# Self-attention over four images on one core: exponentials without a shift, taken straight from PSUM, and the next image's projection woven between the pairs

## The chip, the cores and the metric

The kernel runs on one core of one Trainium2 chip. The metric is the device time of one execution in microseconds (us). The engines are named as the profile names them: PE is TensorE's matmul side and PEld its weight loads, DVE is VectorE, ACT is ScalarE, POOL is GpSimd, SP is SyncE, which here only issues DMAs.

## What is computed

For each of B = 4 images of 64 x 64 pixels with 256 channels, in float32:

```python
q = einsum('bwhc,cd->bwhd', x, Wq) + bq      # d = 128
k = einsum('bwhc,cd->bwhd', x, Wk) + bk      # d = 128
v = einsum('bwhc,cd->bwhd', x, Wv) + bv      # d = 256
pq, pk, pv = (t.reshape(B, -1, N) for t in (q, k, v))   # N = 4096
energy = einsum('bcn,bcm->bnm', pq, pk)      # 4096 x 4096 per image
attention = softmax(energy, axis=-1)
out = einsum('bcm,bnm->bcn', pv, attention).reshape(x.shape)
return gamma * out + x
```

The reshapes do not transpose: an image's flat memory is cut into 128 rows (256 for v) of 4096 columns.

## The kernel before

An image's 4096 query columns n are cut into 8 groups of 512, and the 4096 key columns m into 32 blocks of 128. Two neighbouring blocks are a pair, so that there are 16 pairs in a group and 128 in an image (`STEPS`), 512 in all. The kernel's functions, with their lines:

- `project` (L107) makes pq, pk and pvT of one image in 16 steps. A step turns four 128 x 128 pieces of x (`transposed`, L119), copies them to SBUF on ACT (xts, L123), multiplies them by Wq and Wk (qk, L134), adds the biases on DVE (L142), multiplies by Wv in two halves (v, L152), and after each half lets ACT add the bias while it copies (pvT, L159). All four images do this ahead of their pairs; pq, pk and pvT have one buffer each.
- `energy` (L184) computes one pair's energies, transposed, 128 m by 512 n in each of two banks (s, L188), and ACT copies them to SBUF (p, L196).
- `running_max` (L206) and `column_max` (L210) find the largest energy of each n: a running maximum over the 16 pairs on DVE, then four transposes (mt, L216), a reduction (L218), a diagonal (L220), and a matmul with ones that spreads the result over all partitions (sb, L228), which ACT copies (shift, L232).
- `exponent` (L234) subtracts the shift on DVE in place (L237) and takes the exponential on ACT in place (L240).
- `running_sum` (L242) adds up the exponentials on DVE (ssum, L250), `attend` (L252) multiplies them by pvT into two accumulators (o, L263).
- `finish` (L273) copies the accumulators (L277, L278), adds the two halves of ssum (z, L280), spreads the sum with a matmul of ones (zb, L283), takes reciprocals (L287), scales (L290), and lets POOL add x (L293); SP loads that x (xr) and stores the result (L294).

The order of the work is written out by hand (L296 to L318), and every engine works through its own list in order. Since a group's maximum needs all its energies, energies run `LEAD` = 18 pairs ahead of attention: an image begins with 18 pairs of energies alone, then each step issues energies 18 pairs ahead, the exponential two pairs ahead, the sum, the maximum, and attention. `column_max` and `finish` are generators; `proceed` pushes each of them on by one piece twice in a step. A float32 matmul stands in the trace as two MATMUL instructions.

Of the kernel before, what the change touches and what calls it, by code (L numbers as in the profile page):

```python
# [8 lines left out]
F32 = mybir.dt.float32  # L9
AF = mybir.ActivationFunctionType  # L10
# [6 lines left out]
def kernel(  # L17
# [25 lines left out]

    nc = tc.nc
    B, W, H, C = x.shape
    P = 128
# [7 lines left out]
    KC = C // P  # L54
    STEPS = NG * NP
    LOOK = 2
    LEAD = NP + LOOK
# [11 lines left out]
    xpool = ctx.enter_context(tc.tile_pool(name="xpool", bufs=2))  # L69
    rpool = ctx.enter_context(tc.tile_pool(name="rpool", bufs=2))  # L70
    qkv = ctx.enter_context(tc.tile_pool(name="qkv", bufs=1))
    ppool = ctx.enter_context(tc.tile_pool(name="ppool", bufs=LEAD + 2))
    xtpool = ctx.enter_context(tc.tile_pool(name="xtpool", bufs=2))
    work = ctx.enter_context(tc.tile_pool(name="work", bufs=1))
    stat = ctx.enter_context(tc.tile_pool(name="stat", bufs=2))
    ps_s = ctx.enter_context(tc.tile_pool(name="ps_s", bufs=2, space=PSUM))
    ps_t = ctx.enter_context(tc.tile_pool(name="ps_t", bufs=2, space=PSUM))
    ps_o = ctx.enter_context(tc.tile_pool(name="ps_o", bufs=1, space=PSUM))

    ctx.enter_context(tc.manual_schedule())  # L80

    def load_x(b, g):
        t = xpool.tile([P, 2, NB], F32, tag="x", name=f"x_{b}_{g}")
        nc.sync.dma_start(t, xv[b, g])
        return t

    first = [load_x(0, 0)]
# [19 lines left out]
    def project(b, xs):  # L107
        pq = qkv.tile([P, NM, P], F32, tag="pq", name=f"pq_{b}")
        pk = qkv.tile([P, NM, P], F32, tag="pk", name=f"pk_{b}")
        pvT = qkv.tile([P, NM, C], F32, tag="pvT", name=f"pvT_{b}")  # L110
        def transposed(i):

            g, o = i // 2, (i % 2) * C
            if i % 2 == 0 and len(xs) == g + 1 < NG:
                xs.append(load_x(b, g + 1))
            tp = ps_t.tile([P, KC, 2, P], F32, tag="t", name=f"xt_{b}_{i}")
            for k in range(KC):
                for s in range(2):
                    nc.tensor.transpose(  # L119
                        tp[:, k, s, :], xs[g][:, s, o + k * P : o + (k + 1) * P], ident  # L120
                    )
            xt = xtpool.tile([P, KC, 2, P], F32, tag="xt", name=f"xts_{b}_{i}")
            nc.scalar.copy(xt, tp)  # L123
            return xt

        following = transposed(0)
        for i in range(NM // 2):
            xt = following
            if i + 1 < NM // 2:
                following = transposed(i + 1)  # L130
            qk = ps_s.tile([P, 2, 2 * C2], F32, tag="s", name=f"qk_{b}_{i}")
            for s in range(2):
                for k in range(KC):
                    nc.tensor.matmul(  # L134
                        qk[:, s, :],
                        xt[:, k, s, :],
                        wqk_sb[:, k, :],
                        start=(k == 0),
                        stop=(k == KC - 1),
                    )  # L140
            for dst, o in ((pq, 0), (pk, C2)):
# [7 lines left out]
            vp = ps_o.tile([P, KC, C], F32, tag=f"o{i % 2}", name=f"v_{b}_{i}")  # L149
            for eh in range(KC):  # L150
                for k in range(KC):
# [3 lines left out]
                        xt[:, k].rearrange("p s a -> p (s a)"),  # L155
                        start=(k == 0),
                        stop=(k == KC - 1),
                    )
                nc.scalar.activation(  # L159
                    pvT[:, 2 * i + eh, :],  # L160
# [4 lines left out]
        return pq, pk, pvT  # L165

    for b in range(B):
        pq, pk, pvT = project(b, first)
        pqf = pq.rearrange("p j d -> p (j d)")
        pairs = {}  # L170
        shift = {}
        ssum = {}
# [10 lines left out]

        def energy(step):  # L184
            g, t = divmod(step, NP)
            sp = ps_s.tile([P, 2, NB], F32, tag="s", name=f"s_{b}_{step}")
            for h in range(2):
                nc.tensor.matmul(  # L188
                    sp[:, h, :],
                    pk[:, 2 * t + h, :],  # L190
                    pqf[:, g * NB : (g + 1) * NB],
                    start=True,
                    stop=True,
                )
            p = ppool.tile([P, 2, NB], F32, tag="p", name=f"p_{b}_{step}")
            nc.scalar.copy(p, sp)  # L196
            pairs[step] = p

        def running_max(step):
            g, t = divmod(step, NP)  # L200
            p = pairs[step]
            if t == 0:
                running_max.mx = work.tile([P, 2, NB], F32, tag="mx", name=f"mx_{b}_{g}")
            else:
                q = pairs[step - 1] if t == 1 else running_max.mx
                nc.vector.tensor_tensor(running_max.mx, q, p, ALU.max)  # L206
            if t == NP - 1:
                start(column_max(g, running_max.mx))

        def column_max(g, mx):  # L210
            m1 = work.tile([P, NB], F32, tag="m1", name=f"m1_{b}_{g}")
            nc.vector.tensor_tensor(m1, mx[:, 0, :], mx[:, 1, :], ALU.max)
            yield
            tp = ps_t.tile([P, NJ, P], F32, tag="t", name=f"mt_{b}_{g}")
            for j in range(NJ):
                nc.tensor.transpose(tp[:, j, :], m1[:, j * P : (j + 1) * P], ident)  # L216
            cm = stat.tile([P, NJ], F32, tag="cm", name=f"cm_{b}_{g}")
            nc.vector.tensor_reduce(cm, tp, AX.X, ALU.max)  # L218
            diag = work.tile([P, NJ, P], F32, tag="m1", name=f"diag_{b}_{g}")
            nc.vector.tensor_tensor(  # L220
                diag,
                ident.unsqueeze(1).to_broadcast([P, NJ, P]),
                cm.unsqueeze(2).to_broadcast([P, NJ, P]),
                ALU.mult,
            )
            yield
            sb = ps_t.tile([P, NB], F32, tag="t", name=f"sb_{b}_{g}")
            nc.tensor.matmul(  # L228
                sb, ones, diag.rearrange("p j n -> p (j n)"), start=True, stop=True
            )  # L230
            shift[g] = stat.tile([P, NB], F32, tag="shift", name=f"shift_{b}_{g}")
            nc.scalar.copy(shift[g], sb)  # L232

        def exponent(step):  # L234
            g, t = divmod(step, NP)
            p = pairs[step]
            nc.vector.tensor_tensor(  # L237
                p, p, shift[g].unsqueeze(1).to_broadcast([P, 2, NB]), ALU.subtract
            )
            nc.scalar.activation(p, p, AF.Exp)  # L240

        def running_sum(step):  # L242
            g, t = divmod(step, NP)
            p = pairs[step]
            if t == 0:
                ssum[g] = work.tile([P, 2, NB], F32, tag="ssum", name=f"ssum_{b}_{g}")
            elif t == 1:
                nc.vector.tensor_tensor(ssum[g], pairs[step - 1], p, ALU.add)  # L248
            else:
                nc.vector.tensor_tensor(ssum[g], ssum[g], p, ALU.add)  # L250

        def attend(step):  # L252
            g, t = divmod(step, NP)
            if t == 0:
                attend.acc = [
# [3 lines left out]
            p = pairs[step]  # L259
            for h in range(2):  # L260
                m = 2 * t + h
                for s in range(2):
                    nc.tensor.matmul(  # L263
                        attend.acc[s],
                        pvT[:, m, s * P : (s + 1) * P],
                        p[:, h, :],
# [3 lines left out]
            if t == NP - 1:  # L270
                start(finish(g, attend.acc))

        def finish(g, acc):  # L273
# [6 lines left out]
            nc.vector.tensor_tensor(z, ssum[g][:, 0, :], ssum[g][:, 1, :], ALU.add)  # L280
            yield
            zb = ps_t.tile([P, NB], F32, tag="t", name=f"zb_{b}_{g}")
            nc.tensor.matmul(zb, ones, z, start=True, stop=True)  # L283
            r = work.tile([P, NB], F32, tag="r", name=f"r_{b}_{g}")
# [4 lines left out]
            for s in range(2):  # L289
                nc.vector.scalar_tensor_tensor(  # L290
                    o[:, s, :], o[:, s, :], gam, r, ALU.mult, ALU.mult
                )
            nc.gpsimd.tensor_tensor(xr, xr, o, ALU.add)  # L293
            nc.sync.dma_start(ov[b, g], xr)  # L294

        for step in range(LEAD):  # L296
            energy(step)
            running_max(step)
            proceed()
        while active:  # L300
            proceed()
        exponent(0)
        exponent(1)
        for step in range(STEPS):
            if step + LEAD < STEPS:
                energy(step + LEAD)
            proceed()
            if step + 2 < STEPS:
                exponent(step + 2)
            running_sum(step)  # L310
            if step + LEAD < STEPS:
                running_max(step + LEAD)
            attend(step)
            proceed()
            if step == STEPS - NP and b + 1 < B:
                first = [load_x(b + 1, 0)]
# [32 lines left out]
```

## Time and profile before

| | |
|---|---|
| median of 3 runs | 3162.92 us (3161.79 to 3163.8) |
| the profiled execution | 3163.9 us, span 3162.1 us |
| mean granted clock of TensorE | 0.990 |
| HBM traffic over the span | 34.21 MB read, 16.78 MB written, 16 GB/s |

The span runs from the first to the last instruction; the time lies 1.8 us above it. Granted clock is the share of full speed that TensorE was given. A row of the profile names the line, the engine, the operation, what it writes and reads, the shape, how often, and after a bar the busy time, the mean of one in ns and the idle time of that engine just before it. In a timeline a row is: start, length, engine, line, and in brackets the idle time before it and who ended it.

### The profile page before, as it was taken

Reading aid. Unit: us, or ns where it says so; the run is one execution under the profiler, and the core shown is the slowest. Engines: PE = TensorE matmul, PEld = TensorE weight load, DVE = VectorE, ACT = ScalarE, POOL = GpSimd, SP = SyncE. Lnnn points to the kernel's source line nnn. Section 1 sums busy time; section 2 is a strip of 40 time slices with the busy share of each in tenths; the row PEclk is TensorE's granted clock in tenths of the full one; section 3 lists DMA queues with packets and bytes.
Section 4 is the critical chain, followed back from the end, with each engine's and each line's share of the span. In section 5 each row is a group of like instructions: output and inputs, shape, how many; then the busy total and the mean of one; then the engine's idle time right before and its main releaser. Section 6 shows DMA issues by size and latency. Waiting matters only on the chain.

```text
span 3162.1 us, 20027 instructions
## 1 busy us (share of the span) xinstructions
PE 3006.7 (95%) x7680; PEld 1424.0 (45%) x7680; DVE 2070.7 (65%) x1889; ACT 1158.0 (37%) x1281; POOL 149.9 (5%) x38
## 2 busy tenths in 40 slices
PE   8999999999899999999989999999998999999998
PEld 6444444444644444444464444444446444444443
DVE  1577777776167777777715777777771677777776
ACT  3433333332243333333224333333322433333332
POOL 0000000000000000000000000000000000000000
PEclk9999999999999999999999999999999999999999
DMA  2000000000100000000010000000001000000000
GB/s 69 1 13 10 4 14 14 14 14 20 60 1 14 14 0 14 13 14 14 20 60 0 14 14 0 14 14 13 14 20 60 0 14 13 14 0 14 14 14 20
DMA packets 27743, 52.26 MB, mean 17 GB/s; under 512 B 2048, under 2 KB 3072, under 8 KB 27648
## 3 DMA queue, kind: packets, MB, share of 16 engines
q1 hardware_dynamic: 26112, 50.34, 5.0%
q8 instruction: 60, 0.98, 0.1%
q10 hardware_dynamic: 1536, 0.66, 0.1%
q14 instruction: 35, 0.29, 0.0%
HBM read 34.21 MB, written 16.78 MB: 16 GB/s over the span
## 4 chain that ended last, share of the span: by engine, by line
PE 94%; DVE 3%; ACT 1%; DMA 1%; issue 0%; POOL 0%; POOLq 0%; SPq 0%; DVEq 0%; ACTq 0%
PE o L263 56%; PE s L188 28%; PE v L152 4%; PE qk L134 4%; PE zb L283 1%; PE sb L228 1%; ACT pvT L159 1%; PE xt L119 1%; DVE osb L278 1%; DMA x<-in_x_dram 1%; DVE z L280 1%; PE mt L216 0%; DVE r L287 0%; DVE mx L206 0%; ACT p L196 0%
## 5 line engine op out<-in xcount | busy, mean ns | idle before, releaser
L263 PE MATMUL o<-p,pvT 128*128 128x512 f32 x4096 | 1837.5, 594 | 11.5 <-ACT p L240 11.5
L263 PEld LDWEIGHTS o<-p,pvT 128*128 128x128 f32 x4096 | 780.2, 191 | 996.0 <-issue 981.3
L196 ACT COPY p<-s 128x1024 f32<-128x1024 f32 x512 | 518.2, 1012 | 1430.7 <-PE s L188 1417.8
L188 PE MATMUL s<-pq,pk 128*128 128x512 f32 x2048 | 957.3, 595 | 0.0
L206 DVE TENSOR_TENSOR mx<-mx,p 128x1024 f32<-128x1024 f32 x448 | 565.2, 1262 | 526.4 <-ACT p L196 523.6
L237 DVE TENSOR_TENSOR p<-p,shift 128x1024 f32<-128x1024 f32 x512 | 621.8, 1216 | 52.7 <-ACT shift L232 52.7
L240 ACT ACTIVATE p<-p 128x1024 f32<-128x1024 f32 x512 | 542.5, 1060 | 204.2 <-DVE p L237 200.6
L188 PEld LDWEIGHTS s<-pq,pk 128*128 128x128 f32 x2048 | 388.7, 191 | 477.2 <-issue 460.5
L250 DVE TENSOR_TENSOR ssum<-ssum,p 128x1024 f32<-128x1024 f32 x448 | 546.0, 1219 | 0.8
L293 POOL TENSOR_TENSOR xr<-xr,osb 128x1024 f32<-128x1024 f32 x32 | 149.2, 4661 | 3007.7 <-DVE osb L290 3007.7
L142 DVE TENSOR_TENSOR pq<-qk,bqk_sb 128x256 f32<-128x256 f32 x64 | 27.2, 425 | 270.5 <-PE qk L134 270.5
L152 PE MATMUL v<-xts,wv_sb 128*128 128x256 f32 x512 | 139.0, 394 | 36.1 <-ACT pvT L159 36.1
L159 ACT ACTIVATE pvT<-v,bv_sb 128x256 f32<-128x256 f32 x128 | 60.8, 475 | 210.4 <-PE v L152 210.4
L287 DVE RECIPROCAL r<-zb 128x256 f32<-128x256 f32 x64 | 107.8, 1726 | 40.7 <-PE zb L283 40.7
L134 PE MATMUL qk<-wqk_sb,xts 128*128 128x256 f32 x512 | 126.5, 392 | 0.2 <-ACT xts L123 0.2
L152 PEld LDWEIGHTS v<-xts,wv_sb 128*128 128x128 f32 x512 | 93.0, 191 | 72.2 <-ACT pvT L159 61.8
L134 PEld LDWEIGHTS qk<-wqk_sb,xts 128*128 128x128 f32 x512 | 96.3, 198 | 12.0 <-ACT xts L123 0.6
L206 DVE TENSOR_TENSOR mx<-p,p 128x1024 f32<-128x1024 f32 x32 | 39.2, 1225 | 69.5 <-ACT p L196 69.5
L278 DVE COPY osb<-o 128x512 f32<-128x512 f32 x32 | 22.1, 692 | 94.2 <-PE o L263 94.2
L283 PE MATMUL zb<-z,ones 128*128 128x512 f32 x64 | 35.2, 631 | 48.9 <-DVE z L280 48.9
L248 DVE TENSOR_TENSOR ssum<-p,p 128x1024 f32<-128x1024 f32 x32 | 75.8, 2368 | 0.0
L119 PE MATMUL xt<-ident,x 128*128 128x128 f32 x256 | 40.8, 285 | 28.9 <-DMA x<-in_x_dram 26.9
(23 smaller groups left out, 360.9 us busy)
## 6 DMA issues: line engine op xcount, KB each, us to landing
x<-in_x_dram SPq DMA_DIRECT2D x32, 512.0 KB, 4.0
xr<-in_x_dram SPq DMA_DIRECT2D x32, 512.0 KB, 4.6
out_dram<-xr SPq DMA_DIRECT2D x32, 512.0 KB, 3.5
wv_sb<-in_L_conv_Wv_dram ACTq DMA_DIRECT2D x1, 256.0 KB, 6.9
wqk_sb<-in_L_conv_Wq_dram ACTq DMA_DIRECT2D x1, 128.0 KB, 2.2
wqk_sb<-in_L_conv_Wk_dram ACTq DMA_DIRECT2D x1, 128.0 KB, 5.0
bqk_sb<-in_L_conv_bq_dram ACTq DMA_DIRECT2D x1, 64.0 KB, 6.5
bqk_sb<-in_L_conv_bk_dram ACTq DMA_DIRECT2D x1, 64.0 KB, 6.1
```

The costliest lines, as they stand in the source:

```text
L134: nc.tensor.matmul(qk[:, s, :], xt[:, k, s, :], wqk_sb[:, k, :], start=(k == 0), stop=(k == KC - 1),)
L152: nc.tensor.matmul(vp[:, eh, :], wv_sb[:, k, eh * P : (eh + 1) * P], xt[:, k].rearrange("p s a -> p (s a)"), start=(k == 0), stop=(k == KC ...
L159: nc.scalar.activation(pvT[:, 2 * i + eh, :], vp[:, eh, :], AF.Identity, bias=bv_sb[:, eh : eh + 1],)
L188: nc.tensor.matmul(sp[:, h, :], pk[:, 2 * t + h, :], pqf[:, g * NB : (g + 1) * NB], start=True, stop=True,)
L196: nc.scalar.copy(p, sp)
L206: nc.vector.tensor_tensor(running_max.mx, q, p, ALU.max)
L237: nc.vector.tensor_tensor(p, p, shift[g].unsqueeze(1).to_broadcast([P, 2, NB]), ALU.subtract)
L240: nc.scalar.activation(p, p, AF.Exp)
L250: nc.vector.tensor_tensor(ssum[g], ssum[g], p, ALU.add)
L263: nc.tensor.matmul(attend.acc[s], pvT[:, m, s * P : (s + 1) * P], p[:, h, :], start=(m == 0), stop=(m == NM - 1),)
L287: nc.vector.reciprocal(r[:, sl], zb[:, sl])
L293: nc.gpsimd.tensor_tensor(xr, xr, o, ALU.add)
```

## The change

The new kernel makes four edits to the order and adds a second path.

1. `energy` takes the exponential of the unshifted energies on ACT, from PSUM into p. The copy, the maximum, the subtraction and `column_max` are gone; energies run `LOOK` = 2 pairs ahead; p has 5 buffers for 20.
2. Projection becomes a class. Image 0 is projected whole; images 1 to 3 in pieces (four transposes and the copy; qk and its adds; v and its activations), one after attention of each pair whose number in the image is 2, 4 or 6 modulo 7, so 48 pieces in 112 of 128 pairs. pq, pk and pvT have two buffers. All projection tiles use `ps_t` in PSUM (two slots), as zb does. Both halves of v come ahead of both activations. The pairs of all four images run through as one loop.
3. `finish` gives its matmul later by one piece, keeps the lowest and highest sum in zmin and zmax, scales in one instruction, and stores from POOL's queue.
4. After the pairs a flag is made: is a sum under 2^-60 or over 2^80? If so, a general path (with the maximum, as before, but unwoven) does everything again.

```diff
+    Z_LOW, Z_HIGH = 2.0**-60, 2.0**80
...
-            p = ppool.tile([P, 2, NB], F32, tag="p", name=f"p_{b}_{step}")
-            nc.scalar.copy(p, sp)
+            p = ppool.tile([P, 2, NB], F32, tag="p", name=f"p_{step}")
+            nc.scalar.activation(p, sp, AF.Exp)
...
         def v(self, i):
             pool, tag = self.psum
             vp = pool.tile([P, KC, C], F32, tag=tag, name=f"v_{self.b}_{i}")
             for eh in range(KC):
                 for k in range(KC):
                     nc.tensor.matmul(...)
+            for eh in range(KC):
                 nc.scalar.activation(
                     self.pvT[:, 2 * i + eh, :], vp[:, eh, :], AF.Identity, ...)
...
+        def whole(self):
+            self.transposed(0)
+            for i in range(NI):
+                if i + 1 < NI:
+                    self.transposed(i + 1)
+                self.qk(i)
+                self.v(i)
+
+        def pieces(self):
+            for i in range(NI):
+                self.transposed(i)
+                yield
+                self.qk(i)
+                yield
+                self.v(i)
+                yield
...
+        xpool, rpool, xtpool = pool("xpool", 2), pool("rpool", 2), pool("xtpool", 2)
+        qkv, ppool, work = pool("qkv", 2), pool("ppool", LOOK + 3), pool("work", 1)
+        ps_s = pool("ps_s", 2, space=PSUM)
+        ps_t = pool("ps_t", 2, space=PSUM)
+        ps_o = pool("ps_o", 1, space=PSUM)
...
             nc.vector.tensor_tensor(z, ssum[:, 0, :], ssum[:, 1, :], ALU.add)
             yield
+            yield
             zb = ps_t.tile([P, NB], F32, tag="t", name=f"zb_{b}_{g}")
             nc.tensor.matmul(zb, ones, z, start=True, stop=True)
+            yield
+            nc.vector.tensor_tensor(zmin, zmin, zb, ALU.min)
+            nc.vector.tensor_tensor(zmax, zmax, zb, ALU.max)
...
             nc.gpsimd.tensor_tensor(xr, xr, o, ALU.add)
-            nc.sync.dma_start(ov[b, g], xr)
+            nc.gpsimd.dma_start(ov[b, g], xr)
...
+        for step in range(LOOK):
+            energy(step)
+        for step in range(B * STEPS):
+            r = step % STEPS
+            if r == 0:
+                ahead = following(step // STEPS + 1)
+            if step + LOOK < B * STEPS:
+                energy(step + LOOK)
+            proceed()
+            running_sum(step)
+            attend(step)
+            proceed()
+
+            if r % 7 in (2, 4, 6):
+                next(ahead, None)
+        while active:
+            proceed()
+
+    zs = const.tile([P, 2], F32, name="zs")
+    nc.vector.tensor_reduce(zs[:, 0:1], zmin, AX.X, ALU.min)
+    nc.vector.tensor_reduce(zs[:, 1:2], zmax, AX.X, ALU.max)
+    nc.vector.tensor_scalar(zs[:, 0:1], zs[:, 0:1], Z_LOW, None, ALU.is_lt)
+    nc.vector.tensor_scalar(zs[:, 1:2], zs[:, 1:2], Z_HIGH, None, ALU.is_gt)
+    nc.vector.tensor_tensor(again, zs[:, 0:1], zs[:, 1:2], ALU.add)
+
+    with tc.If(nc.values_load(again[0:1, 0:1]) > 0), ExitStack() as general:
...
```

Three places show how the instructions move. First TensorE at the end of image 0's first group (o is an accumulator, s the energies, zb the spread sum, p_15 or p_654 the group's last pair). Before:

```order
L263 MATMUL o_0_0_601<-p_15_558,pvT_114 128x512
L263 MATMUL o_0_0_602<-p_15_558,pvT_114 128x512
L283 MATMUL zb_0_824<-z_0_822,ones 128x512
L188 MATMUL s_34_828<-pq_112,pk_113 128x512 x2
L263 MATMUL o_0_1_838<-p_16_575,pvT_114 128x512
L263 MATMUL o_0_1_839<-p_16_575,pvT_114 128x512
```

and now:

```order
L259 MATMUL o_0_0_483<-p_654,pvT_114 128x512
L259 MATMUL o_0_0_484<-p_654,pvT_114 128x512
L229 MATMUL s_695<-pq_112,pk_113 128x512 x2
L280 MATMUL zb_0_700<-z_0_693,ones 128x512
L259 MATMUL o_0_1_703<-p_671,pvT_114 128x512
L259 MATMUL o_0_1_704<-p_671,pvT_114 128x512
```

The zb matmul moved behind the next pair's energies. Second, TensorE where image 1 is projected (xt the transposed pieces of x, qk and v the products). Before, ahead of all of image 1's pairs:

```order
L283 MATMUL zb_7_2386<-z_7_2384,ones 128x512
L119 MATMUL xt_0_2400<-ident,x_0_2276 128x128 x4
L119 MATMUL xt_1_2407<-ident,x_0_2276 128x128 x4
L134 MATMUL qk_0_2414<-wqk_sb,xts_0_2405 128x256 x4
L152 MATMUL v_0_2421<-xts_0_2405,wv_sb 128x256 x4
L119 MATMUL xt_2_2430<-ident,x_1_2398 128x128 x4
L134 MATMUL qk_1_2437<-wqk_sb,xts_1_2412 128x256 x4
```

and now, between the pairs of image 0:

```order
L259 MATMUL o_0_0_484<-p_580,pvT_114 128x512
L130 MATMUL xt_1_607<-ident,x_0_512 128x128 x4
L229 MATMUL s_614<-pq_112,pk_113 128x512 x2
...
L229 MATMUL s_624<-pq_112,pk_113 128x512 x2
...
L259 MATMUL o_0_0_484<-p_600,pvT_114 128x512
L145 MATMUL qk_1_634<-wqk_sb,xts_1_612 128x256 x4
L229 MATMUL s_641<-pq_112,pk_113 128x512 x2
```

Two pairs of energies and attention now lie between a piece and the next. Third, SyncE's list of DMAs where image 1's x is loaded (x_0_2276 and x_0_512 are its first tiles, xr the x that is added to the result). Before:

```order
L294 DMA out_dram<-xr_6_2251 256x1x512
L84 DMA x_0_2276<-in_x_dram 128x2x512
L275 DMA xr_7_2379<-in_x_dram 128x2x512
L294 DMA out_dram<-xr_7_2379 256x1x512
L84 DMA x_1_2398<-in_x_dram 128x2x512
L84 DMA x_2_2428<-in_x_dram 128x2x512
```

and now:

```order
L76 DMA x_7_367<-in_x_dram 128x2x512
L76 DMA x_0_512<-in_x_dram 128x2x512
L76 DMA x_1_514<-in_x_dram 128x2x512
L271 DMA xr_0_688<-in_x_dram 128x2x512
L76 DMA x_2_713<-in_x_dram 128x2x512
L76 DMA x_3_901<-in_x_dram 128x2x512
```

The second x tile stood behind image 0's last output; now the outputs are in POOL's list, and both first tiles stand right behind image 0's own.

More of the change, by code (lines that the diff above doesn't have):

```diff
@@ L68, with load_x @@
     const = ctx.enter_context(tc.tile_pool(name="const", bufs=1))
[L69 to L83, printed above, removed]
+    def load_x(pool, b, g):
+        t = pool.tile([P, 2, NB], F32, tag="x", name=f"x_{b}_{g}")
         nc.sync.dma_start(t, xv[b, g])
         return t
-    first = [load_x(0, 0)]
     ident = const.tile([P, P], F32, name="ident")
@@ L164, in project @@
                 )
[L165 to L172, printed above, removed]
+        def whole(self):
[13 more added lines that the diff above has]
+                yield
+    with ExitStack() as fast:
+        fast.enter_context(tc.manual_schedule())
+        pool = lambda name, bufs, **kw: fast.enter_context(
+            tc.tile_pool(name=name, bufs=bufs, **kw)
+        )
+        xpool, rpool, xtpool = pool("xpool", 2), pool("rpool", 2), pool("xtpool", 2)
[3 more added lines that the diff above has]
+        ps_o = pool("ps_o", 1, space=PSUM)
         active = []
@@ L182, in proceed @@
                     active.remove(pieces)
+        pairs, acc, ssum = {}, {}, {}
+        images = [Projection(0, xpool, xtpool, qkv, (ps_t, "t"))]
+        images[0].whole()
         def energy(step):
-            g, t = divmod(step, NP)
-            sp = ps_s.tile([P, 2, NB], F32, tag="s", name=f"s_{b}_{step}")
+            b, r = divmod(step, STEPS)
+            g, t = divmod(r, NP)
+            pr = images[b]
+            sp = ps_s.tile([P, 2, NB], F32, tag="s", name=f"s_{step}")
             for h in range(2):
@@ L204, in running_max @@
             else:
[L205 to L244, printed above, removed]
-            if t == 0:
[L246 to L250, printed above, removed]
@@ L263, in attend @@
                     nc.tensor.matmul(
-                        attend.acc[s],
-                        pvT[:, m, s * P : (s + 1) * P],
-                        p[:, h, :],
+                        acc["now"][s],
+                        images[b].pvT[:, m, s * P : (s + 1) * P],
+                        pairs[step][:, h, :],
                         start=(m == 0),
@@ L300 @@
         while active:
             proceed()
[L302 to L316, printed above, removed]
```

198 lines of the change are left out of this document (152 added, 46 removed).

## Prediction

> **What bounds the kernel now.** I read the page's busy shares first, then the busy time by windows inside a stretch of pairs, then TensorE's timeline across one image boundary, then the waits, and last the timelines of the start and the end. The page's first part (busy us, share of the span, instructions):
>
> ```profile
> PE 3006.7 (95%) x7680; PEld 1424.0 (45%) x7680; DVE 2070.7 (65%) x1889; ACT 1158.0 (37%) x1281; POOL 149.9 (5%) x38
> ```
>
> TensorE leads, but an average does not say whether the last 5% is spread or bunched. Two windows of 100 us in image 0's pairs (PE, PEld, DVE, ACT, POOL busy, then the granted clock):
>
> ```profile
> 300.00:400.00 100.00, 98.46 (x233) 43.42 (x232) 76.62 (x66) 38.81 (x40) 11.02 (x2) 1.00 0.07 21
> ...
> 600.00:700.00 100.00, 98.46 (x233) 43.41 (x233) 72.19 (x63) 38.80 (x40) 7.75 (x1) 1.00 0.03 11
> ```
>
> Inside the pairs TensorE is full at clock 1.00, and VectorE and ScalarE have room. What can be won there is little; it must lie at the boundaries. TensorE's timeline from the last group of image 0 (start, length, line, how often, idle time before):
>
> ```profile
> 784.52 1.12 PE L283 MATMUL zb<-z,ones 128*128 128x512 f32 x2 [1.45 <-DVE z L280]
> ...
> 798.83 1.09 PE L119 MATMUL xt<-ident,x 128*128 128x128 f32 x4 [7.13 <-DMA x<-in_x_dram]
> 799.71 3.62 PE L134 MATMUL qk<-wqk_sb,xts 128*128 128x256 f32 x8
> 803.13 1.58 PE L152 MATMUL v<-xts,wv_sb 128*128 128x256 f32 x4
> ...
> 806.24 0.60 PE L119 MATMUL xt<-ident,x 128*128 128x128 f32 x4
> 806.68 1.89 PE L134 MATMUL qk<-wqk_sb,xts 128*128 128x256 f32 x8
> 808.41 1.03 PE L152 MATMUL v<-xts,wv_sb 128*128 128x256 f32 x4
> 810.00 1.13 PE L152 MATMUL v<-xts,wv_sb 128*128 128x256 f32 x4 [0.56 <-ACT pvT L159]
> 810.97 0.60 PE L119 MATMUL xt<-ident,x 128*128 128x128 f32 x4
> ...
> 902.66 0.66 PE L216 MATMUL mt<-ident,m 128*128 128x128 f32 x4 [3.09 <-DVE m L212]
> 903.15 3.54 PE L188 MATMUL s<-pq,pk 128*128 128x512 f32 x4
> 906.49 1.10 PE L228 MATMUL sb<-diag,ones 128*128 128x512 f32 x2
> ...
> 913.89 5.17 PE L263 MATMUL o<-p,pvT 128*128 128x512 f32 x8 [2.87 <-ACT p L240]
> 918.89 1.88 PE L188 MATMUL s<-pq,pk 128*128 128x512 f32 x4
> 920.61 3.60 PE L263 MATMUL o<-p,pvT 128*128 128x512 f32 x8
> 924.04 1.88 PE L188 MATMUL s<-pq,pk 128*128 128x512 f32 x4
> ...
> 982.41 3.60 PE L263 MATMUL o<-p,pvT 128*128 128x512 f32 x8
> 985.85 0.60 PE L216 MATMUL mt<-ident,m 128*128 128x128 f32 x4
> 986.28 1.88 PE L188 MATMUL s<-pq,pk 128*128 128x512 f32 x4
> 988.00 1.08 PE L228 MATMUL sb<-diag,ones 128*128 128x512 f32 x2
> 988.92 3.60 PE L263 MATMUL o<-p,pvT 128*128 128x512 f32 x8
> ...
> 999.20 1.10 PE L283 MATMUL zb<-z,ones 128*128 128x512 f32 x2 [1.54 <-DVE z L280]
> ```
>
> Starts, not lengths, give the price, since each printed length runs about 0.17 us into the next group (1.89 printed, 1.73 from 806.68 to 808.41). A pair costs 5.15 us (918.89 to 924.04; twelve pairs from 920.61 to 982.41 take 61.80): 1.72 for the energies, 3.43 for attention. A qk block costs 1.73, four transposes 0.44, a two-instruction ones-matmul 0.92 (988.00 to 988.92) or, at the pairs' rate, 5.15 x 2/12 = 0.86. One projection step takes 4.73 (806.24 to 810.97), of which about 0.44 + 1.73 + 1.73 = 3.90 is work. After the gaps the same instructions run slow: 5.00 instead of 3.43 after 2.87 us idle, 3.34 instead of 1.72 after 3.09, qk 3.42 instead of 1.73 after 7.13. TensorE's waits in all (us, times, longest):
>
> ```profile
> PE zb L283 <- DVE z L280: 48.9, 32, 1.5
> ...
> PE v L152 <- ACT pvT L159: 36.1, 64, 0.6
> ...
> PE xt L119 <- DMA x<-in_x_dram: 26.9, 4, 7.2
> ...
> PE mt L216 <- DVE m L212: 12.4, 4, 3.1
> ...
> PE o L263 <- ACT p L240: 11.5, 4, 2.9
> ...
> PE sb L228 <- DVE diag L220: 6.0, 4, 1.5
> ```
>
> So TensorE's own instructions set the end, plus 142 us of waits and what the slowed clock after them costs.
>
> **The change part by part.** It leaves TensorE 512 pairs, 64 projection steps and 32 zb. I build the new span from those.
>
> *Start to first energy.* The rows for image 0's first and last work ahead of the pairs:
>
> ```profile
> 5.27 1.94 PE L119 MATMUL xt<-ident,x 128*128 128x128 f32 x8 [5.27 <-DMA x<-in_x_dram]
> ...
> 82.98 27.63 PE L188 MATMUL s<-pq,pk 128*128 128x512 f32 x64
> ```
>
> Image 0 is still projected whole. Both pvT activations now stand behind all of v, and qk of the next step needs v's PSUM slot (both tiles rotate through ps_t's two slots). The half-way gap of 0.73 (v's four slots end at 808.41 + 0.86 = 809.27, the second half starts at 810.00) becomes one gap after v with two activations in it, about 0.73 + 0.46 = 1.19, and the next transposes run inside it: 3.46 + 1.19 = 4.65 a step for 4.73. I take 82 us to the first energy; bounds 75 (no gap at 15 steps, some 0.5 each) and 84.
>
> *Pairs.* 512 x 5.15 = 2636.8. The removed max, subtraction and second pass over p were VectorE's and ScalarE's, neither of which TensorE waited for here, so they give nothing. The exponential from PSUM isn't in this trace; its nearest rows are the copy it replaces and the exponential from SBUF:
>
> ```profile
> L196 ACT COPY p<-s 128x1024 f32<-128x1024 f32 x512 | 518.2, 1012 | 1430.7 <-PE s L188 1417.8
> ...
> L240 ACT ACTIVATE p<-p 128x1024 f32<-128x1024 f32 x512 | 542.5, 1060 | 204.2 <-DVE p L237 200.6
> ```
>
> 1.01 to 1.06 us in a pair of 5.15, needed by attention two pairs later: no cost. With no column max before it, attention of pair 0 needs only exp(0), which ends some 1.3 us after its energies while TensorE does energies 1 and 2 (3.4 us). That removes mt and sb from every group (32 x (0.44 + 0.92)) and the 3.09, 2.87 and sb waits.
>
> *Projections of images 1 to 3.* 48 steps x 3.90 = 187, in 144 pieces. The cover for the xts copy, the pq/pk adds and the pvT activations is the two pairs (10 us) between pieces; without it a piece would wait as v does now, 0.56. VectorE and ScalarE orders put these behind the exponential of the pair ahead or the running sum, whose results TensorE needs a pair or more later. Changing between long and short matmuls costs 0.00 (mt) to 0.06 (sb) in the rows above; 144 x 0 to 0.06 = 0 to 9, I take 3. The x loads stand on SyncE ahead of use by more than ten pairs, no longer behind an output, and the landing is short beside that:
>
> ```profile
> x<-in_x_dram SPq DMA_DIRECT2D x32, 512.0 KB, 4.0
> ```
>
> The 7.13 goes for three images.
>
> *zb.* It now stands behind the next pair's energies. z is ready 0.16 + 1.54 = 1.70 after attention's last slot, energies take 1.72: the wait of 1.5 goes, 32 x 1.5, with nothing to spare; should VectorE be 0.3 late, 10 us come back. 31 x 0.9 = 28 for the matmuls ahead of the last. zmin and zmax hold zb's slot 1.4 us longer; the next tile but one is a pair or more away.
>
> *The end.* VectorE, Pool and SyncE after the last matmuls:
>
> ```profile
> 3148.29 0.69 DVE L278 COPY osb<-o 128x512 f32<-128x512 f32 x1 [14.90 <-PE o L263]
> 3148.89 0.68 DVE L280 TENSOR_TENSOR z<-ssum 128x512 f32<-128x512 f32 x1
> ...
> 3150.79 3.37 DVE L287 RECIPROCAL r<-zb 128x256 f32<-128x256 f32 x2 [1.22 <-PE zb L283]
> ...
> 3155.81 2.34 POOL L293 TENSOR_TENSOR xr<-xr,osb 128x1024 f32<-128x1024 f32 x1 [53.41 <-DVE osb L290]
> 3158.18 0.59 SPq L294 DMA_DIRECT2D out_dram<-xr  x1
> ```
>
> Attention's last slot ends at about 3148.0, so the tail is 3162.1 - 3148.0 = 14.1. zmin, zmax and the first reduction join the chain at 0.69 each, 2.1. The output issued by Pool isn't in this trace: between SyncE's 0.59 (no difference) and another Pool pass of 2.34, so 0 to 1.8; I take 1, nearer the issue. Loading the flag and branching over the general path isn't either: from nothing, since it runs while the output lands, to one landing of 4.0; I take 2. Tail 19. [...]
>
> Sum: 82 + 2636.8 + 187 + 3 + 28 + 19 = 2956 span. The profiled execution took 3163.9 for a span of 3162.1; its time is 1.0 above the median. So 2956 + 1.8 - 1.0 = **2957 us**, 206 less. Backwards: zb 48.9, x 26.9 - 5.3 = 21.6, v for three images 27, mt, o and sb waits 29.9, mt and sb work 43.5, slow clock 4 x (1.6 + 1.6) + 3 x 2.7 = 21, and 0.17 for each of some 92 waits (they are counted from printed ends) 16: 208, less 5 for the tail, 203. The two agree to 3 us.
>
> **The rivals.** *Pieces stall TensorE.* It works in order, so a piece whose ps_t slot, xts or x tile is late stops the pairs too. At the 0.56 of the v row each, 144 x 0.56 = 81: 3038 us. For it: ps_t now serves xt, qk, v and zb in two slots. Against: in ten microseconds the longest reader chain, zmin to the second reciprocal, is 1.4 + 3.4. It would take 1.4 us for every piece to lose the whole gain.
>
> [...]
>
> *The guard fires.* Then the change doesn't do what it says: general path and fast path both run, about 2957 + 3163, over 6100 us. It decides as soon as one sum leaves 2^-60 to 2^80. From the reference's inputs the sums of unshifted exponentials lie between 2^27 and 2^69; and as each lower bound starts from 1, only 2^80 is near.
>
> **How the numbers follow.** Forecast 0.90, stalls 0.07, clock 0.02, guard 0.01. A change of 0.2% (6 us) is about what can be told from none. The forecast's own ends: down, no switching cost (-3), zb at 0.86 (-1), the tail as now plus its 2.1 (-3), the projection's 75 in part (-5): 2945. Up: switching at 0.06 (+6), tail (+3), zb late (+10), the 48 qk pieces waiting half of 0.56 (+13): 2989. The range is 2945 to 2989; stalls at every piece, clock and guard stay outside with 0.10. Faster 0.96, within 0.2% 0.01 (stalls near 1.4 us each), slower 0.03.
>
> **What would show it.** Right: from the first pair to the last, windows with TensorE above 98% at clock 1.00; pairs of 5.15, with a piece 5.15 + 1.73; waits of TensorE under 15 us outside image 0's projection; no mt or sb; zb after energies with a wait under 0.1; a tail near 19. Wrong: TensorE waiting for ACT xts, ACT pvT or DVE pq between pairs, a clock below 1.00 late in the span, or records of the general path's lines.

## The result and the profile after

| | before | after |
|---|---|---|
| median of 4 runs | 3163.36 us (3161.79 to 3164.53) | 2952.32 us (2950.75 to 2952.38) |
| ratio, 95% interval | | 0.9332 (0.9316 to 0.9348) |
| the profiled execution's span | 3162.1 us | 2949.0 us |
| mean granted clock of TensorE | 0.990 | 0.997 |

The forecast was 2957 us (2945 to 2989); measured are 211 us less than before, forecast were 206. The page's first part of the new kernel, to be laid beside the one in the prediction:

```profile
PE 2919.5 (99%) x7488; PEld 1398.9 (47%) x7488; DVE 903.8 (31%) x840; ACT 634.0 (21%) x737; POOL 123.0 (4%) x70
```

TensorE's share rose from 95% to 99%, VectorE's fell from 65% to 31%, ScalarE's from 37% to 21%. Whether TensorE is full everywhere is asked of windows from the first pairs to the last (PE, PEld, DVE, ACT, POOL busy, then the clock):

```profile
100.00:600.00 500.00, 500.00 (x1302) 242.38 (x1301) 149.22 (x143) 109.45 (x129) 18.88 (x10) 1.00 0.05 18
600.00:1100.00 500.00, 500.00 (x1279) 238.82 (x1279) 157.58 (x144) 108.73 (x126) 23.29 (x12) 1.00 0.04 15
...
2600.00:2900.00 300.00, 300.00 (x701) 132.50 (x700) 102.47 (x83) 61.00 (x62) 15.73 (x8) 1.00 0.03 13
```

No gap is left, and the clock is 1.00 in the last window as in the first. TensorE's timeline from the end of image 0's projection into the first pairs, and at the first group's end:

```profile
72.05 0.60 PE L130 MATMUL xt<-ident,x 128*128 128x128 f32 x4
73.14 1.99 PE L145 MATMUL qk<-wqk_sb,xts 128*128 128x256 f32 x8 [0.49 <-ACT pvT L173]
74.97 1.89 PE L165 MATMUL v<-xts,wv_sb 128*128 128x256 f32 x8
76.70 1.89 PE L145 MATMUL qk<-wqk_sb,xts 128*128 128x256 f32 x8
78.42 1.89 PE L165 MATMUL v<-xts,wv_sb 128*128 128x256 f32 x8
80.15 5.31 PE L229 MATMUL s<-pq,pk 128*128 128x512 f32 x12
85.30 3.60 PE L259 MATMUL o<-p,pvT 128*128 128x512 f32 x8
...
109.77 1.89 PE L145 MATMUL qk<-wqk_sb,xts 128*128 128x256 f32 x8
111.50 1.88 PE L229 MATMUL s<-pq,pk 128*128 128x512 f32 x4
...
173.77 1.88 PE L229 MATMUL s<-pq,pk 128*128 128x512 f32 x4
175.49 1.02 PE L280 MATMUL zb<-z,ones 128*128 128x512 f32 x2
176.34 3.60 PE L259 MATMUL o<-p,pvT 128*128 128x512 f32 x8
```

Attention of pair 0 follows the third energies at once; a qk piece between pairs takes 1.73 (109.77 to 111.50), zb 0.85, and neither has a wait in brackets. Of the waits (us, times, longest) these are left to TensorE:

```profile
PE qk L145 <- ACT pvT L173: 6.9, 14, 0.5
...
PE xt L130 <- DMA x<-in_x_dram: 5.0, 1, 5.0
...
PE zb L280 <- DVE z L276: 1.4, 1, 1.4
```

That is 13 us where 142 stood, all of it ahead of the first pair and at the end.

### The profile page after: what moved, and what is told of

Same layout as the page of the kernel before. It is cut to its first block, busy times and chain, and to the rows that moved or that the text cites. A ratio compares the mean times of both kernels' runs of the same rounds, so it can differ in the third digit from the quotient of the medians.

```text
span 2949.0 us, 17974 instructions
## 1 busy us (share of the span) xinstructions
PE 2919.5 (99%) x7488; PEld 1398.9 (47%) x7488; DVE 903.8 (31%) x840; ACT 634.0 (21%) x737; POOL 123.0 (4%) x70
## 4 chain that ended last, share of the span: by engine, by line
PE 99%; ACT 0%; DVE 0%; DMA 0%; POOL 0%; issue 0%; POOLq 0%; ACTq 0%; DVEq 0%
PE o L259 60%; PE s L229 30%; PE qk L145 4%; PE v L165 4%; PE zb L280 1%; PE xt L130 1%; ACT pvT L173 0%; DMA x<-in_x_dram 0%; DVE r L287 0%; POOL xr L297 0%; ACT L138 0%; DVE osb L289 0%; DVE osb L274 0%; DVE zmin L282 0%; DVE z L276 0%
## 5 line engine op out<-in xcount | busy, mean ns | idle before, releaser
L237 ACT ACTIVATE p<-s 128x1024 f32<-128x1024 f32 x512 | 524.4, 1024 | 1852.6 <-PE s L229 1852.6
L246 DVE TENSOR_TENSOR ssum<-ssum,p 128x1024 f32<-128x1024 f32 x448 | 597.0, 1333 | 1059.8 <-ACT p L237 1047.4
L297 POOL TENSOR_TENSOR xr<-xr,osb 128x1024 f32<-128x1024 f32 x32 | 100.3, 3135 | 2809.7 <-DVE osb L289 2809.7
L274 DVE COPY osb<-o 128x512 f32<-128x512 f32 x32 | 22.1, 691 | 338.8 <-PE o L259 338.8
L165 PE MATMUL v<-xts,wv_sb 128*128 128x256 f32 x512 | 121.0, 379 | 0.0
L173 ACT ACTIVATE pvT<-v,bv_sb 128x256 f32<-128x256 f32 x128 | 53.7, 471 | 247.8 <-PE v L165 247.8
L138 ACT COPY xts<-xt 128x512 f32<-128x512 f32 x64 | 37.4, 586 | 132.5 <-PE xt L130 132.5
L130 PEld LDWEIGHTS xt<-ident,x 128*128 128x128 f32 x256 | 32.5, 143 | 31.7 <-issue 30.3
L289 DVE SCALAR_TENSOR_TENSOR osb<-osb,gam,r 128x1024 f32<-128x1024 f32 x32 | 40.7, 1273 | 0.0
L246 DVE TENSOR_TENSOR ssum<-p,p 128x1024 f32<-128x1024 f32 x32 | 37.2, 1163 | 5.5 <-ACT p L237 5.5
L282 DVE TENSOR_TENSOR zmin<-zmin,zb 128x512 f32<-128x512 f32 x32 | 22.0, 688 | 47.4 <-PE zb L280 47.4
```

The lines of the kernel that those rows point to most:

```text
L130: nc.tensor.transpose(tp[:, k, s, :], self.xs[g][:, s, o + k * P : o + (k + 1) * P], ident,)
L165: nc.tensor.matmul(vp[:, eh, :], wv_sb[:, k, eh * P : (eh + 1) * P], self.xt[i][:, k].rearrange("p s a -> p (s a)"), start=(k == 0), stop= ...
L173: nc.scalar.activation(self.pvT[:, 2 * i + eh, :], vp[:, eh, :], AF.Identity, bias=bv_sb[:, eh : eh + 1],)
L237: nc.scalar.activation(p, sp, AF.Exp)
L246: nc.vector.tensor_tensor(ssum["now"], q, pairs[step], ALU.add)
L289: nc.vector.scalar_tensor_tensor(o, o, gam, r.unsqueeze(1).to_broadcast([P, 2, NB]), ALU.mult, ALU.mult,)
```

## The experiments

E1 to E6 undo one thing in the new kernel or put one back, E7 leaves out its guard, E8 shortens its start and its end, E9 to E11 make single edits in the kernel before, and E12 makes all three of them. Each time is the median of 4 runs; the ratios are to the kernel before, run on the same chip in the same session. Differences to the new kernel are to its 2952.32, which comes from a session of its own; the kernel before moved by up to 2 us between sessions (3163.36 to 3165.47), so a difference of less than that says nothing.

**E1: projections whole, ahead of each image**

```diff
-            if r == 0:
-                ahead = following(step // STEPS + 1)
+            if r == STEPS - LOOK and step + LOOK < B * STEPS:
+                images.append(Projection(step // STEPS + 1, xpool, xtpool, qkv, (ps_t, "t")))
+                images[-1].whole()
...
-            if r % 7 in (2, 4, 6):
-                next(ahead, None)
```

> The new kernel with the projections of images 1 to 3 whole, each in one block ahead of its image's first energies, instead of in pieces. My theory (TensorE's own instructions set the end, weaving only removes the projection's internal waits): a step costs 4.65 instead of 3.89, with 15 such gaps an image 45 x 0.76 = 34, and 0.85 at each start for the first copy, 3: 2952 + 37 = 2989 us. The rival, that weaving carries most of the gain because it removes the image boundary altogether (x wait 7.1, slow clock, two gaps): some 30 to 40 us more an image, 3050 or above.

Measured: 2985.5 us, ratio 0.9433 (0.9417 to 0.9448), 33 more than the new kernel. The one wait that grew by more than 1 us:

```profile
PE qk L145 <- ACT pvT L173: 27.5, 56, 0.5
```

56 waits for 14: 42 x 0.76 = 32. An image has 14 of these gaps (of its 16 qk the first and the last have none); I had said 15. Weaving is worth 33 us, a sixth of the gain. Nearly all of that is the wait for ps_t's two slots, which E8 removes in image 0 without weaving; whether more slots would have served images 1 to 3 as well was not run.

**E2: zb directly behind attention**

```diff
             yield
-            yield
             zb = ps_t.tile([P, NB], F32, tag="t", name=f"zb_{b}_{g}")
```

> The new kernel with one yield fewer in finish, so that zb stands directly behind the group's last attention, as before the change. My theory: each of 31 zb waits 1.61 us for z again, 50 us: 3002 us. The rival, that z is early now since VectorE is at 31% and no longer 65%, so that the place of zb hardly matters: under 15 us, 2952 to 2967.

Measured: 3005.52 us, ratio 0.9496 (0.948 to 0.9511), 53 more. TensorE's waits and the first group's end:

```profile
PE zb L279 <- DVE z L276: 46.3, 32, 1.5
```

```profile
171.34 3.60 PE L259 MATMUL o<-p,pvT 128*128 128x512 f32 x8
176.32 1.12 PE L279 MATMUL zb<-z,ones 128*128 128x512 f32 x2 [1.38 <-DVE z L276]
177.28 1.88 PE L229 MATMUL s<-pq,pk 128*128 128x512 f32 x4
```

Reckoned from start to start, attention ends at 171.34 + 3.43 = 174.77; zb starts 1.55 later and takes 0.96, not 0.85: 31 x 1.66 = 51. One yield in a generator, a line that the change's description hardly shows, carries a quarter of the gain. An idle VectorE doesn't help: z stands in its list behind the copy of an accumulator (L274), and that copy needs the last attention. As data z needs only the running sum, which is done earlier: at the end of the new kernel's trace the sum is ready at 2922.6 and z starts at 2931.3. Whether z ahead of the copy would do as well as the yield was not run.

**E3: the three passes back**

```diff
-            nc.scalar.activation(p, sp, AF.Exp)
+            nc.scalar.copy(p, sp)
...
+        def exponent(step):
+            p = pairs[step]
+            nc.vector.tensor_tensor(p, p, zero.unsqueeze(1).to_broadcast([P, 2, NB]), ALU.subtract)
+            nc.scalar.activation(p, p, AF.Exp)
```

> The new kernel with the three passes over p back: copy from PSUM on ScalarE, subtraction on VectorE (of a tile of zeros), exponential on ScalarE in place; no maximum. My theory: both engines work beside TensorE with two pairs of lead, so nothing changes, 2952 within 3 us. The rival, that freeing ScalarE and VectorE is what made TensorE dense: the chain of 1.0 + 1.2 + 1.1 us makes attention wait, half a microsecond or more a pair, over 3200 us at 0.5 and 2990 or more if only the pairs beside a piece or a finish suffer.

Measured: 2951.83 us, ratio 0.9325 (0.931 to 0.9341). The page's first part:

```profile
PE 2920.8 (99%) x7488; PEld 1399.5 (47%) x7488; DVE 1466.2 (50%) x1353; ACT 1164.9 (39%) x1249; POOL 97.6 (3%) x70
```

562 us more of VectorE and 531 us more of ScalarE, and no difference in time that can be measured. The edit that names the change gains nothing by what it saves on these engines.

**E4: a maximum that nobody uses**

```diff
+        def running_max(step): ...
+        def column_max(g, mx):
+            m1 = work.tile([P, NB], F32, tag="m1", name=f"m1_{g}")
+            nc.vector.tensor_tensor(m1, mx[:, 0, :], mx[:, 1, :], ALU.max)
...
+            for j in range(NJ):
+                nc.tensor.transpose(tp[:, j, :], m1[:, j * P : (j + 1) * P], ident)
...
+            nc.tensor.matmul(sb, ones, diag.rearrange("p j n -> p (j n)"), start=True, stop=True)
...
             running_sum(step)
+            if step >= 1:
+                running_max(step - 1)
```

> The new kernel with a running maximum over p and the column maximum's transposes and ones-matmul back in 31 of 32 groups, placed three pairs behind the group's end; the result is not used. My theory: only TensorE's own work counts, 31 x (0.43 + 0.86 to 0.92) = 40 to 42: 2993 us. Rival: the chain itself (maximum, transposes, reduction, diagonal, matmul) is what costs, with waits of 1 to 3 us a group on TensorE: 3025 to 3090.

Measured: 2991.81 us, ratio 0.9452 (0.9437 to 0.9468), 39.5 more, 1.27 a group: the price of four transposes and a matmul of ones. Its waits are those of the new kernel. So in the new order the maximum costs TensorE its own instructions and nothing else. Here nothing needed its result; in the kernel before, energies run out ahead of an image's last column maximum, and sb waits 1.5 there (717.51 us in its trace), as it does in E11 below.

**E5: the three pieces in a row**

```diff
-            if r % 7 in (2, 4, 6):
-                next(ahead, None)
+            if r % 7 == 4:
+                for _ in range(3):
+                    next(ahead, None)
```

> The new kernel with a projection step's three pieces directly behind each other after one pair in seven, so that no pair lies between transposes and qk. My theory: the pairs between pieces were the cover for the xts copy; without it qk waits 0.17 + 0.03 + 0.59 + 0.06 = 0.85 at each of 48 steps, 41 us: 2993 us. v follows qk without a wait. The rival, that the pieces need no cover since ScalarE is nearly idle: 2952 within 5 us.

Measured: 3000.69 us, ratio 0.9483 (0.9467 to 0.9499), 48 more. One such step on TensorE and ScalarE:

```profile
110.12 0.60 PE L130 MATMUL xt<-ident,x 128*128 128x128 f32 x4
110.76 0.58 ACT L138 COPY xts<-xt 128x512 f32<-128x512 f32 x1 [2.79 <-PE xt L130]
111.40 1.99 PE L145 MATMUL qk<-wqk_sb,xts 128*128 128x256 f32 x8 [0.68 <-ACT xts L138]
113.23 1.89 PE L165 MATMUL v<-xts,wv_sb 128*128 128x256 f32 x8
```

qk starts 1.28 behind the transposes' start, not 0.43: the 0.85 expected. Then it takes 1.83 (111.40 to 113.23) where it takes 1.73 without a wait. 48 x 0.95 = 46, and three waits of v behind qk's adds, 2.8 us in all, make 48. A piece that needs another engine's result right away does stop TensorE; the pairs between pieces are the cover, and together they hide 48 us.

**E6: stores from SyncE**

```diff
-            nc.gpsimd.dma_start(ov[b, g], xr)
+            nc.sync.dma_start(ov[b, g], xr)
```

> The new kernel with the outputs stored from SyncE's queue again. My theory: the x loads are issued some 14 pairs (70 us) ahead, so an output that waits for Pool ahead of them in the list delays nothing; the end changes by the issue alone: 2952 within 3 us. The rival, that moving the outputs to Pool's queue is what removed TensorE's waits for x: 7.1 us at each of three image starts or at several of the 24 later loads, 2970 to 3100.

Measured: 2959.19 us, ratio 0.935 (0.9335 to 0.9366), 7 more, where I had expected no difference. Its interval overlaps the new kernel's (0.9316 to 0.9348), so the time alone would not settle it; the trace does. SyncE, Pool and TensorE at image 2's first piece, then TensorE at image 3's:

```profile
821.78 3.26 POOL L297 TENSOR_TENSOR xr<-xr,osb 128x1024 f32<-128x1024 f32 x1 [80.00 <-DVE osb L289]
825.07 0.59 SPq L298 DMA_DIRECT2D out_dram<-xr  x1
825.71 1.39 SPq L76 DMA_DIRECT2D x<-in_x_dram  x2
827.19 0.61 SPq L271 DMA_DIRECT2D xr<-in_x_dram  x1
831.88 0.66 PE L130 MATMUL xt<-ident,x 128*128 128x128 f32 x4 [3.32 <-DMA x<-in_x_dram]
832.37 1.88 PE L229 MATMUL s<-pq,pk 128*128 128x512 f32 x4
...
1562.96 0.66 PE L130 MATMUL xt<-ident,x 128*128 128x128 f32 x4 [2.51 <-DMA x<-in_x_dram]
1563.45 3.03 PE L229 MATMUL s<-pq,pk 128*128 128x512 f32 x4
1566.27 4.19 PE L259 MATMUL o<-p,pvT 128*128 128x512 f32 x8
```

My "14 pairs ahead" holds for later tiles. An image's first tile is loaded in the same call that transposes it, so it is early only when SyncE, with nothing to wait for, has run ahead in its list. With the last group's output in front it waits for Pool, and TensorE waits 3.3 us for it, 2.5 at image 3; image 1's first tiles come before any output. Behind the 2.5 the next instructions ran slow (energies 2.82 for 1.72, attention 4.03 for 3.43), 1.7 more. In the profiled execution, whose span is 8.4 longer than the new kernel's, another 1.0 lies ahead of the first energies (81.17 for 80.15), which the stores don't touch. So the move of the stores is a working part of the change, small but not free to leave out.

**E7: no guard.** zmin, zmax, the flag and all behind `zs` are cut.

> The new kernel without zmin and zmax, without the flag and without the general path; the check on the range of the sums is left out. My theory: zmin, zmax and the first reduction go from the end's chain, 0.6 each, and loading the flag and branching, which I put at 2 to 3: 2952 - 4.5 = 2947.5 us. The rival, that the branch runs wholly while the last output lands: 2950.

Measured: 2949.87 us, ratio 0.9323 (0.9307 to 0.9339), at the rival's 2950 rather than at my 2947.5, and not to be told from the new kernel by time. By the traces the end is shorter: from attention's last slot (a slot is the 0.429 us from one matmul instruction's start to the next; 24 of them follow 2920.11 in the new kernel, 15 follow 2924.66 in E7) to the span's end it takes 18.6 us with the guard (2930.4 to 2949.0), 15.5 without (2931.1 to 2946.6). What is fetched at the end fits this. DMA packets from 2935 to 2950 us of the new kernel, by queue (packets, MB, share):

```profile
q0 software_dynamic: 144, 0.52, 9.0%
q14 instruction: 6, 0.05, 1.3%
q8 instruction: 2, 0.03, 1.0%
```

and of E7 from 2930 us on:

```profile
q0 software_dynamic: 144, 0.52, 4.6%
```

With the guard, instructions are fetched while the last output lands. From the output's issue to the end it is 6.8 us (2942.20) with the guard and 5.3 (2941.35) without: the flag and the branch cost 1.5 there, of my 2 (2.4 in E8, whose output is issued at 2931.01 for an end at 2938.7), and zmin, zmax and the reduction the other 1.6, of my 2.1. So the branch does not hide wholly behind the output.

**E8: free slots for image 0**

```diff
-        images = [Projection(0, xpool, xtpool, qkv, (ps_t, "t"))]
+        images = [
+            Projection(
+                0, xpool, xtpool, qkv, (ps_t, "t"), (ps_s, "s"), ((ps_o, "o0"), (ps_o, "o1"))
+            )
+        ]
...
-            nc.vector.tensor_tensor(zmin, zmin, zb, ALU.min)
-            nc.vector.tensor_tensor(zmax, zmax, zb, ALU.max)
...
                 ALU.mult,
             )
+            nc.vector.tensor_tensor(zmin, zmin, zb, ALU.min)
+            nc.vector.tensor_tensor(zmax, zmax, zb, ALU.max)
```

> The new kernel with image 0's qk in ps_s and its v in ps_o, which are free at that time, and with zmin and zmax behind the scaling. My theory: the 14 waits of 0.49 us for ScalarE (0.76 counted by slots, 15 of them) go, 11 us, and 1.2 at the end: 2940 us. The rival, that image 0's projection is bound by the loads of x or by ScalarE anyway: 2950.

Measured: 2940.77 us, ratio 0.9293 (0.9278 to 0.9309), 12 below the new kernel and the fastest of all. Its projection steps of image 0:

```profile
12.52 0.60 PE L132 MATMUL xt<-ident,x 128*128 128x128 f32 x4
12.96 1.89 PE L147 MATMUL qk<-wqk_sb,xts 128*128 128x256 f32 x8
14.69 1.89 PE L167 MATMUL v<-xts,wv_sb 128*128 128x256 f32 x8
16.41 0.60 PE L132 MATMUL xt<-ident,x 128*128 128x128 f32 x4
```

3.89 a step, no wait: the 0.76 a step was the wait for a free slot in ps_t alone, not x and not ScalarE's rate. The first energies start at 70.47 us for 80.15, and attention's last slot to the end takes 18.0 for 18.6, where I had expected 1.2 less.

**E9 to E12: edits in the kernel before.** E9 adds the one yield of the change to its `finish`. E10 loads two tiles of the next image early:

```diff
-                first = [load_x(b + 1, 0)]
+                first = [load_x(b + 1, 0), load_x(b + 1, 1)]
```

E11 leaves out the maximum of each image's first group:

```diff
-        shift = {}
+        shift = {0: zero}
...
-            if t == NP - 1:
+            if t == NP - 1 and g > 0:
                 start(column_max(g, running_max.mx))
...
             running_max(step)
+            if step >= NP:
+                exponent(step - NP)
             proceed()
         while active:
             proceed()
-        exponent(0)
-        exponent(1)
```

E12 makes all three.

> The kernel before with one edit of the change alone: one more yield in finish, so that zb stands behind the next pair's energies in the 6 of 8 groups of an image that still have energies to come. My theory: 24 x 1.6 = 38 us less, 3125 us. The rival, that VectorE at 65% makes z late there, so that zb still waits half: 3144.

> The kernel before with the first two tiles of the next image's x loaded early instead of one, so that the second no longer stands behind an output in SyncE's list. My theory: at three images the wait of 7.1, 0.2 of its matmul's printed end and 2.7 of slow clock go, 30 us: 3134 us. The rival, that the clock falls there anyway or the third tile waits in its place: 3142 to 3155.

> The kernel before without the column maximum of each image's first group (a shift of zero is subtracted there, the exponentials of pairs 0 and 1 stand two pairs ahead of attention). My theory: at each of 4 images the waits of 3.1, 1.5 and 2.9, 0.5 for printed ends, 3.2 of slow clock and 1.4 of matmuls go, 12.6 each: 50 us, 3114 us. The rival, that attention then waits for the exponentials behind the 18 pairs' copies and maxima all the same: 3140 or more.

> The kernel before with the three edits together: zb later, two x tiles early, no maximum in first groups. My theory: the terms add, 38 + 30 + 50 = 118: 3046 us; what is then left to the new kernel is the maximum's matmuls in 28 groups (37), unwoven projections (33) and 8 zb waits (13), less 5 at the end. The rival, that they hide one another (one wait gone lets another end last): 3070 or more.

| | us | ratio, 95% interval | below the 3165.5 of the kernel before |
|---|---|---|---|
| E9 | 3121.52 | 0.9862 (0.9844 to 0.9879) | 44, expected 38 |
| E10 | 3132.55 | 0.9896 (0.988 to 0.9912) | 33, expected 30 |
| E11 | 3122.15 | 0.9863 (0.9845 to 0.988) | 43, expected 50 |
| E12 | 3049.27 | 0.9633 (0.9618 to 0.9648) | 116, expected 118 |

The three gains add up to 120, E12 shows 116, within the intervals: these waits don't hide one another. E9's waits for z are down to those 8 groups that have no energies to follow, from 48.9:

```profile
PE zb L284 <- DVE z L280: 12.0, 8, 1.5
```

E10's only wait for x is image 0's. In E11 two rows are gone (mt, o), but this one stands as before:

```profile
PE sb L231 <- DVE diag L223: 6.0, 4, 1.5
```

I had put it to the first groups and counted 6 us too many; without them the expected gain is 44.

## Why the prediction was right, step by step

- *TensorE's own instructions set the end.* Shown: the windows are full, E3 adds over 500 us each to the other two engines and the time doesn't change, and E4 costs TensorE's instructions alone. But the prediction read its windows of 98.46 as "full" and said that little could be won inside the pairs. Of the 211 us some 80 were won there: the wait for z at 24 groups that have energies behind them (44, E9), 1.5 us a group, which is what each of the two windows lacks, and the maximum's matmuls (36, from E4), which count as busy. The sum had both terms, so the number didn't suffer.
- *Start to first energy.* 82 us forecast, 80.15 measured; a step of image 0 took 4.65 as worked out (11.60 to 16.25 in the new kernel's timeline below), and E8 shows that the cause named, the ps_t slot, was the right one.

```profile
11.60 0.60 PE L130 MATMUL xt<-ident,x 128*128 128x128 f32 x4
...
16.25 0.60 PE L130 MATMUL xt<-ident,x 128*128 128x128 f32 x4
```

- *Pairs, pieces, zb.* Forecast from the first energy to attention's last slot: 2636.8 + 187 + 3 + 28 = 2855. Measured: 2930.4 - 80.15 = 2850. The difference is the 3 for switching between shapes, which was not needed, and zb's 0.85 for 0.9. The cover that I named for the pieces is real: without it, E5, 48 us.
- *zb.* Forecast: the wait goes, with nothing to spare. Right, and E2 and E9 show it from both sides (53 and 44 us).
- *x loads.* The 7.1 at three images went, as forecast, but the step's reason was half right: E6 shows that an image's first tile isn't loaded well ahead by the order, but by a SyncE that has nothing in front of it.
- *The end.* 19 forecast, 18.6 measured, with errors that offset one another: zmin, zmax and the reduction 1.6 for 2.1, flag and branch 1.5 for 2, Pool's store 1.4 for 1 (5.3 from its issue to the end in E7, 3.9 from SyncE's in the kernel before). The end of the new kernel:

```profile
2934.39 3.36 DVE L287 RECIPROCAL r<-zb 128x256 f32<-128x256 f32 x2
2937.67 0.63 DVE L325 TENSOR_REDUCE zs<-zmin 128x1 f32<-128x512 f32 x1
2938.22 1.27 DVE L289 SCALAR_TENSOR_TENSOR osb<-osb,gam,r 128x1024 f32<-128x1024 f32 x1
...
2939.58 2.33 POOL L297 TENSOR_TENSOR xr<-xr,osb 128x1024 f32<-128x1024 f32 x1 [75.06 <-DVE osb L289]
...
2940.30 1.62 DVE L329 TENSOR_TENSOR again<-zs 128x1 int32<-128x1 f32 x1
2942.20 0.68 POOL L298 DMA_DIRECT2D out_dram<-xr  x1 [0.30 <-DVE again L329]
```

Instruction packets, 8 of them with 0.08 MB, stand at the end of the new kernel, and none at that of E7 or of the kernel before; loading the flag, branching and fetching cost 1.5 to 2.4 us together here, under the bound of 4.0 from a landing; what the fetch alone costs no run separates.

- *The backward sum.* The parts, each by a run: zb later 53 (E2), weaving 33 (E1), x early 33 (E10), first groups' maximum 43 (E11), the maximum's matmuls in the other 28 groups 28 x 1.27 = 36 (from E4), the sb waits 6, image 0's projection 3 (82.98 to 80.15), less 4.5 for the end: 202.5 of 211. Missing from this list, as from the forecast's own of 203, is what the new inner order of a projection gives images 1 to 3. Where none of them waits for x, such a projection takes 76.5 us in the old order (E10, 785.40 to 861.89 us) and 73.4 in the new (E1, 738.78 to 812.16), at all three images: 9.3 us, and the sum is 212. That it comes so near is partly chance, since each part is a difference of medians good to 1 or 2 us.
- *The rivals.* None of the three to which the forecast gives a chance came about: stalls, the clock, the guard. Stalls at pieces exist, but only where the cover is taken away (E5) or an image's first x tile comes late (E6). The clock stood at 1.00 in every window from 100 to 2900 us of the new kernel, 2.8 ms without a wait of TensorE. The general path's lines don't occur in the trace.

## What to carry to other kernels

When one engine's own instructions fill its time inside the loop, look for the gain at the loop's edges, and count there what that engine itself issues and waits for: over a thousand microseconds of work put back on engines that nobody waits for cost nothing here (E3), and one generator step between an addition and the matmul that needs it was worth 53 (E2). A busy engine isn't one on which nothing can be won: the maximum's matmuls were part of the 95%. Price by start-to-start times from a stretch without waits; such a sum of instructions came within 0.2% of the measured time. A load that is "early" because its queue happens to be empty isn't early by order: ask what would stand in front of it.

## What the runs showed of the hardware

- The VectorE addition that writes the flag, 128x1, took ten times as long beside a Pool addition, and ended with it: 1.62 us in the new kernel, to 2941.92, with Pool's addition to 2941.91 (2939.58 + 2.33), and 1.61 in E6, to 2950.90, with Pool's to 2950.89 (2948.55 + 2.34). In E8, where Pool had just finished, the same instruction took 0.16:

```profile
2928.37 2.34 POOL L303 TENSOR_TENSOR xr<-xr,osb 128x1024 f32<-128x1024 f32 x1 [75.62 <-DVE osb L293]
...
2930.88 0.16 DVE L335 TENSOR_TENSOR again<-zs 128x1 int32<-128x1 f32 x1
```

What lengthens this addition no run separates. The Pool addition of 128x1024 took from 2340 ns on average (E3) to 4661 (the kernel before), but not by VectorE's share: it was 50% in E3, 65% in the kernel before, and 67% in E9, where the addition took 3099. What VectorE ran beside it in each was not followed up.

- Whether the granted clock fell after a gap of TensorE went by the gap's length, and in the middle it went either way. In the kernel before, the three gaps of 7.1 to 7.2 us were followed by a clock of 0.50 to 0.60 over the next 4 us; of its eight gaps of 2.87 and 3.09 us seven were followed by 0.50 to 0.64, and one, of 2.87, by 1.00. In E6 energies took 2.82 us behind a gap of 2.51, and 1.72 as elsewhere behind one of 3.32. Which of them lose the clock is open; the prediction's sum backwards took all eight of the kernel before, and seven lost it. After gaps of 1.5 it did not fall: the 35 waits of 1.45 to 1.54 ahead of the end of the kernel before were each followed by 1.00 over 4 us; E2, with 32 waits of at most 1.5, has a mean clock of 0.998, the kernel before 0.990, and E10, without the three gaps of 7, 0.995.
- The first matmuls behind a wait cost some 0.10 us extra here (qk 1.83 for 1.73 in E5, zb 0.96 for 0.85 in E2), which no list of waits shows.
